# One core, FFN–attention–FFN: all five engines in source order, side work in small steps, table entries by indirect writes, value products two key tiles at a time

## The chip, the cores and the metric

The kernel runs on one core of one Trainium2 chip. Times are device microseconds (us) of one launch. A profiled execution also gives a trace, in which every instruction of the five engines (TensorE = PE, VectorE = DVE, ScalarE = ACT, GpSimd = POOL, SyncE = SP) has a start and an end.

## The reference, cut to what matters

The input x has 4 batches of 512 tokens and 256 features. One layer is computed, in fp32:

```
x = x + 0.5 * ffn(layernorm(x))
x = x + attention(layernorm(x))
x = x + 0.5 * ffn(layernorm(x))        # the same weights as the first

ffn(x):   logits = x @ gate             # 8 experts
          w, e = top_2(logits); w = softmax(w)
          out = sum over the two e of  w * ((silu(x @ w0[e]) * (x @ w1[e])) @ wo[e])   # 256 -> 512 -> 256

attention(x):   # 16 heads of 64 plain + 64 rotary dimensions
          q   = rms_norm(x @ wq_a) @ wq_b          # rank 64
          c,r = split(x @ wkv_a)                   # rank 64, and 64 rotary dimensions common to all heads
          k,v = split(rms_norm(c) @ wkv_b)
          rope on q's rotary part and on r
          out = softmax(q.k / sqrt(128)) @ v, heads side by side, @ wo
```

## The kernel before

**Three stages.** The first FFN, the attention and the second FFN follow each other. The up and key projections of the heads are folded into the queries and the value projection into the output weights ahead of time (`fold_pieces`), so that keys and values of all heads are the low-rank rows of the batch.

**FFN.** A token and one of its two experts make a pair; there are 4096 pairs. Each expert's pairs are put into slots, 128 slots make a tile of one expert, and 39 tiles (`NTILES`) hold every possible split. A table `tab` (slot within the tile by tile: token and weight) says which pair lies in which slot. To route a batch, the kernel normalises its rows (`norm`, L317), stores them to DRAM (`xn_d`), transposes them, multiplies with the gate, chooses two experts (`top_two`), numbers the slots (`slots`), and adds every pair to the table: for each of 8 groups of 128 pairs, three one-hot tiles (L609 on POOL, L613 on DVE) and a matmul (`put`, L624). `list_pieces` then lists the tiles that are full, and after the last batch the rest. Batches 0 and 1 are routed at the start (`route_first`, with all 16 one-hot groups in `p_put`), which fills `n_a` = 9 tiles; batches 2 and 3 are routed beside these tiles. In the second FFN, batches 0 to 2 are routed beside the attention (17 tiles), and batch 3 beside the first of these.

For each tile `ffn_tiles` (L746) gathers 128 rows by an indirect DMA (L760, POOL), transposes them (L772, to xT by DVE at L775), makes the two hidden products (`hidden`, L790, 8 matmuls; Silu on ACT, product on DVE at L802), transposes that (L808), projects it (L817), scales it by the pair's weight (L827, DVE) and adds it into the result `acc_d` in DRAM by an indirect DMA that accumulates (L832, POOL).

**Attention.** 64 items (batch, head) of 4 query tiles and 4 key tiles (`NT` = 4) each. `before_pieces` (L882) prepares a batch: norm, transposes, rotary keys (L896), low-rank rows (L911) with an RMS norm, and their transposes (L940). `queries` (L952) makes the queries of two heads, with `rope` (L870): two DVE and three POOL operations. `scores` (L966) makes one 128x512 tile of scores on PE (L969), its row maximum on DVE (L977), the exponential with row sums on ACT (L980), the reciprocal on DVE (L981) and the division on POOL (L982). `turn_probs` (L985) transposes the probabilities of one key tile `kc` (L989; copied to SBUF by DVE or ACT in turn). `weigh` (L999) multiplies one key tile of two heads with the values into `po` (L1002, 64 columns wide). `out_project` (L1010) projects two pairs of heads and adds them to x (L1016).

The main loop (L1162 to L1178) goes through items and key tiles. At each it issues the scores five tiles ahead (`LEAD` = 1), the transposes of this tile, and then, by the key tile, a `weigh`, the queries of a later pair, or half an output projection. At `kc` 1 a hook runs a piece of side work: one of the pieces of routing (9 to a batch) or of preparing (6 to a batch).

**What sets the order.** PE and SP run in source order (`manual_schedule(engines={PE, SP})`, L110). DVE, ACT and POOL are ordered by the tile scheduler, which may move an instruction of side work before or behind those of the main work on the same engine. Roots are taken on ACT (L313 for LayerNorm, L922 for RMS norm), which has to load a table of functions between Sqrt and Exp or Silu. DMAs that SP issues stand in one queue: after the first-layer weights it loads wo's weights (L1075, 4 MB), then x of batches 2 and 3 (L1077), `mark_d`, the start of `acc_d`, and the attention's weights (`load_attention`, L227), among them `nwq`, which DVE scales by a constant (L241).

Of the kernel before, what the change touches and what calls it, by code (L numbers as in the profile page):

```python
# [9 lines left out]
F32 = mybir.dt.float32  # L10
# [22 lines left out]
def kernel(  # L33
# [49 lines left out]
    xp = ctx.enter_context(tc.tile_pool(name="xn", bufs=4))  # L83
    lp = ctx.enter_context(tc.tile_pool(name="lT", bufs=1))
    qp = ctx.enter_context(tc.tile_pool(name="q", bufs=3))
    pp = ctx.enter_context(tc.tile_pool(name="p", bufs=2 * NT + LEAD))
    ptp = ctx.enter_context(tc.tile_pool(name="pt", bufs=NT + 2))
    ap = ctx.enter_context(tc.tile_pool(name="o", bufs=2))
    dp = ctx.enter_context(tc.tile_pool(name="dram", bufs=1, space=bass.MemoryType.DRAM))
    ps_a = ctx.enter_context(tc.tile_pool(name="ps_a", bufs=4, space=PSUM))  # L90
    ps_t = ctx.enter_context(tc.tile_pool(name="ps_t", bufs=2, space=PSUM))
    ps_p = ctx.enter_context(tc.tile_pool(name="ps_p", bufs=2, space=PSUM))
# [4 lines left out]

    mark_d = dp.tile([P, n_full(2)], F32, name="mark_d")
# [11 lines left out]
    order = {mybir.EngineType.PE, mybir.EngineType.SP}  # L110
    ctx.enter_context(tc.manual_schedule(engines=order))
# [76 lines left out]
    for t in (xn_d[0], acc_d[0], xn_d[1], acc_d[1]):  # L188
        nc.gpsimd.dma_start(t[NTOK:, :], zero)
# [112 lines left out]

    H2 = NT // 2

    def stats(b):

        mv = small.tile([P, NT, 2], F32, tag="mv", name="mv")
        for t in range(NT):
            sb = small.tile([P, 6], F32, tag="st", name="st")
            nc.vector.bn_stats(sb, xs[b][:, t, :])  # L310
            nc.vector.bn_aggr(mv[:, t, :], sb)
        rstd = small.tile([P, NT], F32, tag="rstd", name="rstd")
        nc.scalar.activation(rstd, mv[:, :, 1], AF.Sqrt, bias=eps_ln)  # L313
        nc.vector.reciprocal(rstd, rstd)
        return mv, rstd

    def norm(b, store=None, alone=False):  # L317

        xt = xs[b]
        mv, rstd = stats(b)  # L320
        if alone:
            less = small.tile([P, NT], F32, tag="less", name="less", bufs=2)
            nc.vector.scalar_tensor_tensor(
                less, mv[:, :, 0], -1.0, rstd, ALU.mult, ALU.mult
            )
        halves = []
        for half in range(2):
            xn = xp.tile([P, H2, D], F32, tag="xn", name="xn")
            for i in range(H2):
                t = half * H2 + i  # L330
                if alone and half:
                    nc.scalar.activation(
                        xn[:, i, :], xt[:, t, :], AF.Identity,
                        bias=less[:, t : t + 1], scale=rstd[:, t : t + 1],
                    )
                    continue
                eng = nc.gpsimd if i and not alone else nc.vector
                eng.tensor_scalar(
                    xn[:, i, :], xt[:, t, :], mv[:, t, 0:1], rstd[:, t : t + 1],
                    ALU.subtract, ALU.mult,  # L340
                )
            if store is not None:
                queue, dst = store
                r0 = b * S + half * H2 * P
                queue.dma_start(
                    dst[r0 : r0 + H2 * P, :].rearrange("(t p) d -> p t d", p=P), xn
                )
            halves.append(xn)
        return halves

    def turn_norm(halves):

        xnT = tp.tile([P, DC, S], F32, tag="xnT", name="xnT")
        for half, xn in enumerate(halves):
            pt = ps_p.tile([P, DC, H2 * P], F32, tag="p", name="pt_ln")
            for c in range(DC):
                for t in range(H2):
                    nc.tensor.transpose(  # L358
                        pt[:, c, t * P : (t + 1) * P], xn[:, t, c * P : (c + 1) * P], ident
                    )  # L360
            nc.scalar.copy(xnT[:, :, half * H2 * P : (half + 1) * H2 * P], pt)
        return xnT


    class Phase:


        def __init__(self, f):
            self.f = f

            self.run = rt.tile([P, NE], F32, name=f"run{f}")
            nc.gpsimd.memset(self.run, 0.0)

            self.tab = rt.tile([P, 2, P], F32, tag="tab", name="tab")
            self.in_a = None

    def own(name, shape, dt=F32, bufs=3):

        return small.tile(shape, dt, tag=name, name=name, bufs=bufs)

    def top_two(ph, pg, nt, mk):


        def bcast(v):
            return v.unsqueeze(2).to_broadcast([P, nt, NE])

        lg = mk("lg", [P, nt, NE], bufs=2)
        nc.vector.tensor_copy(lg, pg[:, :, :NE])
        hot = mk("hot", [P, 2, nt, NE], bufs=2)
        wgt = mk("wgt", [P, 2, nt])  # L390
        tops = []
        for k in range(2):
            m = mk(f"m{k}", [P, nt])
            nc.vector.tensor_reduce(m, lg, AX.X, ALU.max)
            eq = mk("eq", [P, nt, NE], bufs=2)
            nc.vector.tensor_tensor(eq, lg, bcast(m), ALU.is_equal)
            nc.vector.tensor_mul(eq, eq, rank[:, :nt])
            rm = mk("rm", [P, nt])
            nc.vector.tensor_reduce(rm, eq, AX.X, ALU.max)
            nc.vector.tensor_tensor(hot[:, k], eq, bcast(rm), ALU.is_equal)  # L400
            tops.append(m)
            if k == 0:
                lg2 = mk("lg2", [P, nt, NE], bufs=2)
                nc.vector.scalar_tensor_tensor(
                    lg2, hot[:, k], -BIG, lg, ALU.mult, ALU.add
                )
                lg = lg2

        both = mk("both", [P, 2, nt, NE], bufs=2)
        nc.vector.tensor_add(both[:, 0], hot[:, 0], hot[:, 1])  # L410
        nc.vector.tensor_copy(both[:, 1, 0, :], ph.run)
        for t in range(nt):
            nc.vector.tensor_add(
                both[:, 1, t + 1, :] if t + 1 < nt else ph.run,
                both[:, 1, t, :],
                both[:, 0, t, :],
            )

        ex = mk("ex", [P, nt])
        nc.vector.tensor_sub(ex, tops[1], tops[0])  # L420
        nc.scalar.activation(ex, ex, AF.Exp)
        den = mk("den", [P, nt])
        nc.vector.tensor_scalar_add(den, ex, 1.0)
        nc.vector.reciprocal(den, den)

        nc.vector.tensor_scalar_mul(wgt[:, 0], den, 0.5)
        nc.vector.tensor_mul(wgt[:, 1], ex, wgt[:, 0])
        return {"hot": hot, "wgt": wgt, "both": both}

    def slots(s, b, nt, mk):  # L430

        pr = ps_p.tile([P, nt, NE], F32, tag="p", name="pr")
        for i, m in enumerate((below, ones)):
            nc.tensor.matmul(  # L434
                pr.rearrange("p t e -> p (t e)"),
                lhsT=m,
                rhs=s["both"][:, i].rearrange("p t e -> p (t e)"),
                start=(i == 0),
                stop=(i == 1),
            )  # L440
        sv = mk("sv", [P, nt, NE], bufs=2)
        nc.vector.tensor_add(sv, pr, base[:, :nt])
        mine = mk("mine", [P, 2, nt, NE], bufs=2)
        nc.vector.tensor_mul(
            mine, s["hot"], sv.unsqueeze(1).to_broadcast([P, 2, nt, NE])
        )
        sl = mk("sl", [P, 2, nt])
        nc.vector.tensor_reduce(sl, mine, AX.X, ALU.add)
        s_i = mk("s_i", [P, 2, nt], I32)
        nc.vector.tensor_copy(s_i, sl)  # L450
        lo_i = mk("lo_i", [P, 2, nt], I32)
        nc.vector.tensor_single_scalar(lo_i, s_i, P - 1, ALU.bitwise_and)
        hi_i = mk("hi_i", [P, 2, nt], I32)
        nc.vector.tensor_single_scalar(hi_i, s_i, 7, ALU.arith_shift_right)
        lo = mk("lo", [P, 2, nt])
        nc.vector.tensor_copy(lo, lo_i)
        hi = mk("hi", [P, 2, nt])
        nc.vector.tensor_copy(hi, hi_i)
        val = mk("val", [P, 2, nt])
        nc.vector.scalar_tensor_tensor(  # L460
            val, tok_id[:, :, :nt], float(b * S), lo, ALU.add, ALU.subtract
        )
        return {"lo": lo, "hi": hi, "val": val}

    def route_first(ph, queue):

        s = {}
        nt = 2 * NT
        used = [0]

        def scratch(name, shape, dt=F32, bufs=0):
            if "scr" not in s or used[0] + math.prod(shape[1:]) > S:
                s["scr"] = pp.tile([P, S], F32, tag="p", name="scr")
                used[0] = 0
# [11 lines left out]
        def p_norm(b):  # L486
            s["xn", b] = norm(b, (queue, xn_d[ph.f]), True)
# [771 lines left out]
```

## Time and profile before

| | |
|---|---|
| time of 3 runs: median (lowest to highest) | 1213.18 us (1211.97 to 1214.32) |
| time of the profiled execution | 1212.9 us |
| its span (first to last instruction) | 1211.1 us |
| mean granted TensorE clock | 0.979 |
| first FFN: hidden products of tile 0 start at | 43.83 us |
| hidden products of tile 8 start at | 120.58 us |
| attention | about 318 to 968 us |
| second FFN | about 968 us to the end |
| queries to queries, a pair of heads without side work | 16.56 us; with an output projection 19.71 us |

The page gives the busy time of each engine over the whole span and in 40 equal slices, and the chain of instructions that ended last. Timelines give start, duration, engine, line and operation, and in brackets how long the engine had been idle and what released it. "SPq" is the time that an instruction took to be issued by SP's queue, not its transfer. In the trace a transposing matmul is one record and an fp32 matmul with 512 columns two. A block's "slot" below is the time from the start of its first matmul to the start of the next block's, since the ends of matmuls overlap.

### The profile page before, as it was taken

What the parts mean: (1) busy time and instruction counts of PE and PEld (TensorE: products, weight loads), DVE (VectorE), ACT (ScalarE), POOL (GpSimd) and SP (SyncE); (2) the same over time, 40 slices, a digit from 0 to 9 for tenths busy, and PEclk for the clock granted to TensorE, in tenths of its full rate; (3) what the DMA queues carried; (4) which work ended last, traced back from release to release, by engine and by line L of the source; (5) the groups of instructions that cost most, each with busy time, mean ns of one, the idle gap of its engine ahead of it and who ended that gap; (6) DMA issues with size and microseconds to landing.
All of it is one profiled execution on the core that took longest, in us unless ns stands there. A gap on an engine that the chain in (4) does not pass through costs nothing. (4 is left out here: it accounts for less than half of the span.)

```text
span 1211.1 us, 15165 instructions
## 1 busy us (share of the span) xinstructions
PE 1142.1 (94%) x4788; PEld 641.9 (53%) x4788; DVE 611.1 (50%) x1615; ACT 489.1 (40%) x1023; POOL 593.9 (49%) x631
## 2 busy tenths in 40 slices
PE   5599999899899999999999999999999899999996
PEld 4366666566545454445454445544555466666664
DVE  6355222333356565676566685666866435322221
ACT  4341221332355455645556644556544431122111
POOL 3265444455455545456555465455644335344352
PEclk7899999989999999999999999999999999999998
DMA  9941222322100000100001000001000122222431
GB/s 319 367 98 30 44 44 48 70 38 40 20 1 1 1 1 1 53 1 1 1 1 49 4 1 1 1 1 35 1 1 1 45 48 36 44 44 45 113 53 22
DMA packets 40334, 52.12 MB, mean 43 GB/s; under 512 B 9376, under 2 KB 32672, under 8 KB 40160
## 3 DMA queue, kind: packets, MB, share of 16 engines
q0 software_dynamic: 15808, 23.08, 10.8%
q1 hardware_dynamic: 24176, 28.06, 7.2%
q8 instruction: 41, 0.67, 0.2%
q14 instruction: 37, 0.30, 0.1%
q10 hardware_dynamic: 272, 0.01, 0.0%
HBM read 34.09 MB, written 21.24 MB: 46 GB/s over the span
## 5 line engine op out<-in xcount | busy, mean ns | idle before, releaser
L982 POOL TENSOR_SCALAR pr<-pr,sm 128x512 f32<-128x512 f32 x256 | 176.6, 696 | 232.9 <-DVE sm L981 192.9
L790 PE MATMUL h<-w_sb,xT 128*128 x624 | 286.5, 602 | 1.9 <-DVE xT L775 1.5
L969 PE MATMUL ps<-k,q 128*128 128x512 f32 x512 | 275.1, 621 | 0.0
L980 ACT ACTIVATE pr<-ps,nm 128x512 f32<-128x512 f32 x256 | 176.2, 689 | 178.6 <-DVE nm L977 145.5
L989 PEld LDWEIGHTS pt<-ident,pr 128*128 128x128 f32 x1024 | 129.0, 142 | 161.7 <-issue 114.8
L977 DVE TENSOR_REDUCE nm<-ps 128x1 f32<-128x512 f32 x256 | 175.5, 686 | 73.3 <-PE ps L969 72.6
L832 POOL DMA_INDIRECT acc_d<-yo,idx x64 | 101.8, 1590 | 192.9 <-DVE yo L827 176.6
L989 PE MATMUL pt<-ident,pr 128*128 128x128 f32 x1024 | 159.4, 276 | 20.1 <-POOL pr L982 18.3
L790 PEld LDWEIGHTS h<-w_sb,xT 128*128 128x128 f32 x624 | 114.5, 193 | 120.3 <-issue 118.7
L802 DVE TENSOR_TENSOR it<-g,h 128x512 f32<-128x512 f32 x78 | 53.6, 687 | 239.5 <-PE h L790 192.6
L810 ACT COPY iT<-pt_i 128x512 f32<-128x512 f32 x78 | 45.7, 585 | 258.7 <-PE pt_i L808 258.7
L817 PE MATMUL py<-w_sb,iT 128*128 x624 | 147.7, 380 | 0.7 <-ACT iT L810 0.7
L1002 PE MATMUL po<-pT,low 128*64 128x512 f32 x512 | 142.8, 623 | 1.2 <-ACT pT L996 1.2
L969 PEld LDWEIGHTS ps<-k,q 128*128 128x128 f32 x512 | 81.6, 192 | 91.2 <-issue 72.5
L817 PEld LDWEIGHTS py<-w_sb,iT 128*128 128x128 f32 x624 | 112.7, 190 | 14.4 <-issue 1.4
L996 ACT COPY pT<-pt 128x512 f32<-128x512 f32 x128 | 74.7, 583 | 84.9 <-PE pt L989 84.4
L760 POOL DMA_INDIRECT xg<-xn_d,idx x78 | 77.9, 998 | 30.4 <-issue 18.9
L994 DVE COPY pT<-pt 128x512 f32<-128x512 f32 x128 | 87.1, 681 | 10.5 <-PE pt L989 10.5
L800 ACT ACTIVATE g<-h 128x512 f32<-128x512 f32 x78 | 46.6, 597 | 103.5 <-PE h L790 103.4
L981 DVE RECIPROCAL sm<-sm 128x1 f32<-128x1 f32 x256 | 40.9, 160 | 91.5 <-ACT pr L980 91.4
L827 DVE TENSOR_SCALAR yo<-py,wt 128x256 f32<-128x256 f32 x78 | 37.7, 484 | 65.0 <-PE py L817 65.0
L876 POOL TENSOR_TENSOR tsin<-tsin,sin_sb 128x512 f32<-128x512 f32 x36 | 45.7, 1271 | 36.9 <-DVE tsin L875 36.9
(249 smaller groups left out, 1211.4 us busy)
## 6 DMA issues: line engine op xcount, KB each, us to landing
w_sb<-in_L_ffn_w_kernel_dram SPq DMA_DIRECT2D x8, 1024.0 KB, 17.3
w_sb<-in_L_ffn_wo_kernel_dram SPq DMA_DIRECT2D x4, 1024.0 KB, 13.8
x<-_attn_hidden_states_dram SPq DMA_DIRECT2D x4, 512.0 KB, 7.0
xn_d<-xn POOLq DMA_DIRECT2D x8, 256.0 KB, 5.7
x<-acc_d SPq DMA_DIRECT2D x4, 512.0 KB, 3.7
acc_d<-x SPq DMA_DIRECT2D x4, 512.0 KB, 2.9
xn_d<-xn SPq DMA_DIRECT2D x8, 256.0 KB, 2.3
out_dram<-acc_d SPq DMA_DIRECT2D x4, 512.0 KB, 5.7
```

Source lines behind the costliest of these rows:

```text
L760: nc.gpsimd.indirect_dma_start(out=xg[j], out_offset=None, in_=xn_d[f][: res["rows"], :], in_offset=bass.IndirectOffsetOnAxis(ap=res["idx" ...
L790: nc.tensor.matmul(p, lhsT=xT[j][:, c, :], rhs=w_sb[w][:, bass.ds(off + c * MLP, MLP)], start=(c == 0), stop=(c == DC - 1),)
L817: nc.tensor.matmul(py, lhsT=iT[:, m, :], rhs=w_sb[2][:, bass.ds(off + m * D, D)], start=(m == 0), stop=(m == MC - 1),)
L832: nc.gpsimd.indirect_dma_start(out=dst, out_offset=bass.IndirectOffsetOnAxis(ap=idx, axis=0), in_=y, in_offset=None, compute_op=ALU.add,)
L969: nc.tensor.matmul(ps, lhsT=qT[:, t * P : (t + 1) * P], rhs=st[b]["k"][h % 2], start=True, stop=True,)
L977: nc.vector.tensor_reduce(nm, ps, AX.X, ALU.max, negate=True)
L980: nc.scalar.activation(pr, ps, AF.Exp, bias=nm, accum_out=sm)
L982: nc.gpsimd.tensor_scalar(pr, pr, sm, 1.0, ALU.mult, ALU.mult)
L989: nc.tensor.transpose(pt[:, t * P : (t + 1) * P], probs[t][:, kc * P : (kc + 1) * P], ident)
L994: nc.vector.tensor_copy(s, pt)
L996: nc.scalar.copy(s, pt)
L1002: nc.tensor.matmul(po[j * RANK : (j + 1) * RANK], lhsT=st[b]["low"][:, kc, 1, :], rhs=pts[j], start=(kc == 0), stop=(kc == NT - 1),)
```

## The change

All five engines run in source order (`engines=None`). So an instruction of side work stands on each engine exactly where the source issues it, and everything behind it on that engine waits while it waits.

Side work is written as generators that stop after a few instructions; a queue, `Beside`, takes one step at fixed places: four places in a tile of the FFN (before: one), one or two in a key tile of the attention. In the first FFN the routing of batches 2 and 3 takes 3 steps a place beside tiles 0 and 1 and 2 steps beside tiles 2 to 6; what is left is done at the end of tile 6.

```diff
-    order = {mybir.EngineType.PE, mybir.EngineType.SP}
-    ctx.enter_context(tc.manual_schedule(engines=order))
+    ctx.enter_context(tc.manual_schedule(engines=None))
...
     for j in tiles:
-        for f in hooks.pop(j, ()):
-            f()
-        if j == len(jobs) - 1:
-            put_scores(0)
-            put_scores(1)
+        place = place + 1 if place < 4 else 1
+        if j < n_a - 2:
+            beside.step(3 if j < 2 else 2)
+            if j == n_a - 3 and place == 4:
+                beside.finish()
```

Roots: the Sqrt of ACT and the reciprocal become a bit trick with three Newton steps, 11 small DVE operations, for every norm but the first two. Normalised rows are made by DVE and ACT, no longer by POOL.

```diff
+    def inv_sqrt(y, x, n):
+        nc.vector.tensor_single_scalar(
+            y.bitcast(I32), x.bitcast(I32), 1, ALU.arith_shift_right
+        )
+        nc.vector.tensor_scalar(
+            y.bitcast(I32), y.bitcast(I32), -1.0, float(0x5F3759DF), ALU.mult, ALU.add
+        )
+        a = small.tile([P, n], F32, tag="newton", name="newton")
+        for i in range(3):
+            nc.vector.scalar_tensor_tensor(a, y, -0.5, x, ALU.mult, ALU.mult)
+            nc.vector.tensor_mul(a, a, y)
+            nc.vector.scalar_tensor_tensor(y, a, 1.5, y, ALU.add, ALU.mult)
```

The table: a pair's two numbers (8 bytes) go to their slot in a table in DRAM, `tab_d`, by an indirect DMA from POOL, 128 pairs at a time; once all are written, SP reads the table back (128 KB). Batches 0 and 1 of the first FFN keep the 16 one-hot groups; batches 2 and 3 use 8 writes and 8 one-hot groups (all three one-hots on DVE); each batch of the second FFN uses 8 writes.

```diff
+        def scatter(self, s, k, t):
+            nc.gpsimd.memset(self.between, 0.0)
+            put = nc.gpsimd.indirect_dma_start(
+                out=tab_d[self.f],
+                out_offset=bass.IndirectOffsetOnAxis(ap=s["s_i"][:, k, t : t + 1], axis=0),
+                in_=s["pair"][:, k, t, :],
+                in_offset=None,
+            )
```

The attention's loop: `at` counts the 8 key tiles of a pair of heads. `weigh` takes two key tiles at a time; the division is issued at a place of its own; queries and `rope` are taken in steps (`asked`): queries' matmuls at 5, the first rotary DVE operation at 6, the second at 7, and POOL's three at 0 (product), 1 (upper half, behind the division) and 2 (lower half) of the next pair, whose first scores stand at 3.

```diff
+            at = NT * (h % 2) + kc
+            k = (i + 1) * NT + LEAD + kc
+            put_scores(k)
             pts[i, kc] = turn_probs(probs[i], kc)
-            if kc == 0 and h % 2 == 0 and i > 0:
-                put_weigh(i - 1, NT - 1)
-            if kc > 0 and h % 2 == 1:
-                put_weigh(i, kc - 1)
-            if kc == 2 and h % 2 == 1:
-                put_queries((i + 3) // 2)
-            if kc >= 2 and h % 4 == 0 and i > 0:
-                put_out(i - 1, kc - 2)
-            if kc == 1:
-                for f in hooks.pop((b, h), ()):
-                    f()
+            for f in late:
+                f()
+            late.clear()
+            if at == 1 and i > 0:
+                put_weigh(i - 1, (2, 3))
+            elif at == 7:
+                put_weigh(i, (0, 1))
+            elif at == 3 and h % 4 == 0 and i > 1:
+                late.append(put_out(i - 1, 0))
+            elif at == 4 and h % 4 == 1 and i > 1:
+                late.append(put_out(i - 2, 1))
+                late.append(lambda i=i: finish_x(i - 2))
+            elif at == 5:
+                asked.add(put_queries((i + 3) // 2))
+            if kc % 2:
+                beside.step()
+            else:
+                asked.step()
+            put_divide(k)
+            if kc % 2:
+                asked.step()
+                if at in (1, 7):
+                    beside.step()
+            else:
+                beside.step()
```

Smaller edits: the first two score tiles of the attention are no longer issued before the last projection of the first FFN; x of batches 2 and 3 is loaded before wo's weights; the PSUM pool of scores, hidden products and `po` has 3 buffers instead of 4, that of side work 3 instead of 2; SBUF pools are cut anew. The scaling of `nwq`, which in the source stands ahead of the first tile's xT, is not edited; on DVE it now runs at that place.

## The prediction, as put on record

> **What bounds the kernel now.** I read the page's busy shares and slices first, then the waits of PE, then PE's timeline where the slices dip.
>
> ```profile
> PE 1142.1 (94%) x4788; PEld 641.9 (53%) x4788; DVE 611.1 (50%) x1615; ACT 489.1 (40%) x1023; POOL 593.9 (49%) x631
> ...
> PE   5599999899899999999999999999999899999996
> ```
>
> PE is busy 94% of the span and no other engine over 50%. A change can win by taking work off PE or by filling its gaps, and lose by opening new gaps: a 20 us gap costs 1.6%. The dips are slices 1 and 2 and a few single ones. The table of stretches gives the size:
>
> ```profile
> 43.80:120.60 76.80, 64.34 (x273) 39.84 (x274) 38.58 (x160) 20.70 (x32) 36.36 (x37) 0.91 0.47 129
> ...
> 334.00:968.00 634.00, 614.49 (x2666) 311.28 (x2664) 409.26 (x1012) 340.85 (x766) 334.17 (x392) 0.99 0.03 9
> 968.00:1198.00 230.00, 228.88 (x896) 143.42 (x897) 70.87 (x178) 48.94 (x82) 100.45 (x81) 1.00 0.29 53
> ```
>
> (Columns: stretch, length, busy PE, PEld, DVE, ACT, POOL, clock, DMA share, GB/s.) PE idles 12.5 us in tiles 0 to 7 of the first FFN, 19.5 us in the attention, 1.1 us in the second FFN. What ends these gaps:
>
> ```profile
> PE pt L989 <- POOL pr L982: 18.3, 14, 2.8
> PE pt_ln L494 <- DVE xn L338: 9.0, 1, 9.0
> PE pt_ln L358 <- DVE xn L338: 9.0, 1, 9.0
> PE pt_i L808 <- DVE it L802: 8.0, 5, 3.7
> ```
>
> In the attention PE waits for divided probabilities, 14 times up to 2.8 us. One such place, ACT first, then PE:
>
> ```profile
> 505.70 1.28 ACT L313 ACT_TABLE_LOAD   x1
> 507.00 0.30 ACT L313 ACTIVATE rstd<-mv,eps_ln 128x4 f32<-128x4 f32 x1
> 507.31 1.28 ACT L980 ACT_TABLE_LOAD   x1
> 508.61 0.69 ACT L980 ACTIVATE pr<-ps,nm 128x512 f32<-128x512 f32 x1
> ```
> ```profile
> 510.49 0.33 PE L989 MATMUL pt<-ident,pr 128*128 128x128 f32 x1 [2.63 <-POOL pr L982]
> ```
>
> A root costs ACT 2.9 us, the exponentials come late, and PE stands 2.63 us.
>
> **The change part by part**, against the profiled execution's 1212.9 us (the median of the runs, 1213.18, is 0.02% away).
>
> *1. Start of the first FFN.* DVE in source order meets the scaling of `nwq` (L241) right before xT of tile 0. Before, DVE's scheduler put it late:
>
> ```profile
> 43.83 5.37 PE L790 MATMUL h<-w_sb,xT 128*128 x8 [0.60 <-DVE xT L775]
> ```
> ```profile
> 60.08 2.98 SPq L240 DMA_DIRECT2D nwq<-n_L_attn_q_a_norm_w_dram  x2
> ...
> 69.51 0.14 DVE L241 TENSOR_SCALAR nwq<-nwq 128x1 f32<-128x1 f32 x1
> ```
>
> SP issues its two loads at 60 to 63 us, a median 5.2 us before they land: 65 to 68. Behind the scaling on DVE stand xT of tile 0, its product, and all statistics of batch 2; behind xT PE waits. SP's order ahead of `nwq` moves the same bytes, so the loads won't be earlier. Tile 0 starts at about 68.3 instead of 43.8: +24.5. Given back: the old wait of 9.0 us in tile 1 for batch 2 (x landing at 55.7, behind wo's weights) is gone. That leaves about +13 if tiles 0 to 7 otherwise keep pace, which is my lower bound.
>
> I don't expect them to. The routing of two batches and the listing are some 60 steps, 3 or 2 at each of 4 places a tile, ending in tile 6, and PE's part of a step waits in order for DVE's. I walked the emitted order with durations of rows: DVE carries about 31 us of side work (statistics 0.41 + 0.17 a tile of rows, choice 7.5, 24 one-hots at 0.28 to 0.47, table sums, listing), each round a trip PE to DVE and back. The walk puts tile 8 at 148 us against 120.58: +28. It charges every round trip in full, so I take the middle, **+20** (13 to 28). Half of the 16 one-hot groups' matmuls are already off in it.
>
> *2. Rest of the first FFN.* Tiles 8 to 38 at 5.82 us (hidden 3.44, projection 1.73, transposes 0.44 and 0.22) need 180.4; preparing batch 0 takes 6.1 of PE and queries 2.1; together 189. Now they take 318 − 120.6 = 197.4. The two waits at 229 to 247 (stretch: 18.0 us, PE 12.2) stem from Sqrt loads and POOL's rows (1278 ns each) ahead of gathers, which go. In steps, one a place, PE waits little: **−7** (−8 to 0).
>
> *3. Attention.* (a) *Switching to 64-wide matmuls.* In a block of four `po` records the two heads lie side by side in the two halves of the array's columns, so it streams as many columns as one score tile; it takes a slot of 1.01 against the score tile's 0.86; the scores' slot after it is 0.96 instead of 0.86, and the transposes' before it 0.53 instead of 0.44. A visit costs 0.15 + 0.10 + 0.09 = 0.35. One double block stands in the trace, 1.87 instead of 2.02. Four visits a pair become two: 0.70 × 32 pairs = **−22.4** (−16 to −22.4).
>
> (b) *The upper half of the rotary queries.* It now stands on POOL behind the division of tile 1, and the next pair's first scores at tile 3 wait for it. From the start of tile 1's scores: scores 0.6, maximum 0.69, exponential 0.69 + 0.19, reciprocal 0.16, hand-overs of 0.1 to 0.2 each, division 0.70, add 1.27: about 4.8 to 6.8 depending on what DVE holds. PE is there after tile 1 (0.86 + 0.53 + 1.87) and tile 2 (0.96 + 0.44, and waits for tile 2's own chain), about 6.1. I take 0.75 a pair: 32 × 0.75 = **+24** (0 to 35: at most 1.1 a pair). POOL's row for rope's operations:
>
> ```profile
> L876 POOL TENSOR_TENSOR tsin<-tsin,sin_sb 128x512 f32<-128x512 f32 x36 | 45.7, 1271 | 36.9 <-DVE tsin L875 36.9
> ```
>
> (c) *Roots off ACT.* Of the 19.5 us of idle PE most stands around the roots; the row maxima still meet the 11 Newton operations on DVE in order (row L311's 172 ns each, 2 us, in two steps). I take 60% of 21 us (the idle time plus slow clock after it): **−12.6** (−21 to 0).
>
> The Trainium skill, "ScalarE: Activation LUTs", section "What ACT_TABLE_LOAD costs", counts a drain of about 1.38 us with each 1.28 us load; here the exponential follows its load at 507.31 by 1.30 us, so no drain shows. By the page the term could be twice as large; the row decides.
>
> (d) *Table matmuls* of three batches: 12 blocks (L624) with slots of 0.86 to 0.97 go: **−11** (certain as PE time; by idle elsewhere it may be hidden: −11 to 0).
>
> (e) *Indirect writes*: 8 a batch, 24 here. The trace has none of 8 bytes a row. From below the gather's 998 ns of POOL, from above the adding write's 1590:
>
> ```profile
> L832 POOL DMA_INDIRECT acc_d<-yo,idx x64 | 101.8, 1590 | 192.9 <-DVE yo L827 176.6
> ...
> L760 POOL DMA_INDIRECT xg<-xn_d,idx x78 | 77.9, 998 | 30.4 <-issue 18.9 <-DVE off L739 4.8 <-PE po L1002 4.4
> ```
>
> I take 1.4 with its small memset, nearer the write. Queued behind each on POOL are the division and rope; whoever is late there is the next pair's scores. Also, rope's add in a batch's first pairs waits for writes to land (3.8 us for `acc_d` <- `yo`). POOL's busy share in the attention is 53%, so half of it hides: 8 × 1.4 = 11 a batch, of which I charge 5: **+15** (0 to 18).
>
> The skill, "DMA: Bandwidth & Descriptors", table "Specifications", says transfers below 512 bytes are read, modified and written, which speaks against 8-byte writes. No row here has such a transfer; the one other case is the adding write, which also reads first.
>
> (f) *Side steps on DVE in order* hold a row maximum back by about half an operation of 0.69, in 28 of 32 pairs: 0.35 × 28 = **+10** (0 to 10).
>
> (g) *Start.* No scores are issued before the last projection, and five first tiles run max, exp, reciprocal in turn on DVE: now about 6 us are lost at 318 to 334: **+3** (0 to 4).
>
> Attention: −22.4 + 24 − 12.6 − 11 + 15 + 10 + 3 = **+6** (−35 to +30, since not all ends come together).
>
> *4. Second FFN.* Four table blocks of batch 3 go: **−3.5** (−3.5 to 0). Its tiles already run at 5.83, near their floor.
>
> Buffers: the pool of scores with 3 costs nothing by itself in the FFN (two hidden products in use, 3.44 us, freed by 0.69 of DVE); in the attention it is part of (b).
>
> **Sum**: 1212.9 + 20 − 7 + 6 − 3.5 = 1228.4.
>
> **Rivals.**
>
> *A, the other side: the chain behind POOL keeps up.* If the upper half is ready before PE reaches tile 3 (it decides at 6.1 us from tile 1's start; DVE must be free when each maximum comes) and the writes hide in POOL's idle 47%, (b), (e) and (f) vanish: 1228.4 − 24 − 15 − 10 = 1179. For it: POOL idles 193 us before divisions, waiting for DVE, not the reverse. Against: DVE is 65% busy in the attention (409 of 634 us) and in order now.
>
> *B, worse: the chain is late in every pair* and writes cost the upper price: (b) 35, (e) 18, start +28: 1228.4 + 11 + 3 + 8 = 1250.
>
> *C, grouping does nothing:* if slots around a double block pay the switch twice, (a) is 0 and the time is about 1228.4 + 22 = 1250, unless (b) is gone too: 1226.
>
> *D, the hold at the start is not there* (`nwq` lands by 50): 1228.4 − 20 = 1208.
>
> **How the numbers follow.** Forecast and its near surroundings (1210 to 1245): 0.45. A: 0.26. B and C at 1250: 0.20. D: 0.09. The range takes in A's 1179 and B's 1250 with some margin: 1177 to 1256. The likeliest case's own range is 1210 to 1245. 0.2% (2.4 us) is about what a measurement of this kernel can tell from no change. Faster: A and half of D, 0.31; within 0.2%: the rest of D and 0.01 of the forecast's lower end, 0.05; slower: 0.64.
>
> **What would show it.** Right or wrong by the profile of the changed kernel: tile 0's hidden products start at 65 to 70 us, released by DVE's xT, behind `nwq` (else term 1 fails); tile 8 starts at 134 to 149. A clean pair, queries to queries, at 16.4 to 16.6 as before says (a) and (b) cancel; at 15.8 rival A holds; PE's waits would name the rotary queries' upper half at the scores' line with about 24 us. `po` blocks of eight records with slots near 1.87 show (a). No table loads between 330 and 960 but for Exp. The 24 writes show their POOL slot directly. I would be wrong mostly if the in-order DVE is not late at the row maxima.

## The result, and the profile after

The changed kernel is slower: 1306.95 us median (1296.25 to 1309.77, 4 runs) against 1212.58, a ratio of 1.0755 (95% interval 1.0700 to 1.0811). The profiled execution took 1296.25 us (span 1294.5), the fastest of the four; the other three have a mean granted clock of 0.947 to 0.948 instead of its 0.959. A fifth execution on record, not in this median, took 1301.42 us at 0.956.

The page of the changed kernel, busy time and slices:

```profile
PE 1133.8 (88%) x4704; PEld 642.0 (50%) x4704; DVE 617.1 (48%) x1673; ACT 452.2 (35%) x992; POOL 578.2 (45%) x645
...
PE   5367899999889999897989879898879998999996
```

PE has 8.3 us less work than before and 91.7 us more idle time in its span. Slices 2 and 3 are deeper, and dips stand all over the attention. The stretches (columns as in the prediction): tiles 0 to 7, attention, first 17 tiles of the second FFN.

```profile
66.70:153.70 87.00, 66.16 (x252) 39.83 (x253) 37.80 (x148) 15.44 (x26) 28.47 (x33) 0.88 0.20 34
...
346.28:1034.58 688.30, 612.04 (x2632) 318.02 (x2630) 421.33 (x1078) 321.67 (x761) 334.49 (x412) 0.97 0.03 8
1034.58:1150.25 115.67, 106.35 (x414) 65.78 (x414) 37.20 (x122) 24.02 (x40) 47.60 (x46) 0.97 0.30 45
```

| | before | after | difference |
|---|---|---|---|
| start to tile 8 of the first FFN | 120.58 | 153.70 | +33.1 |
| tile 8 to the attention's first scores | 197.55 | 192.58 | −5.0 |
| attention (to the second FFN's first product) | 645.3 | 688.3 | +43.0 |
| second FFN, tiles 0 to 16 | 107.4 | 115.7 | +8.3 |
| its tiles 17 to 38 and the end | 140.2 | 144.2 | +4.0 |

These are the two profiled executions, and the differences come to 83.4 us; of the 94.4 us between the medians, 11 lie in executions without a trace.

The waits of PE name new causes at the top; what led before (PE for the division, 18.3 us) is down to 3.2:

```profile
PE ps L1100 <- POOL q L1001: 56.2, 30, 8.1
PE pt_ln L381 <- DVE xn L367: 23.7, 8, 8.4
PE h L907 <- DVE xT L892: 21.6, 3, 20.5
...
PE pt L1122 <- POOL pr L1116: 3.2, 5, 1.2
```

**The start.** DVE's timeline, then PE's:

```profile
66.03 0.15 DVE L247 TENSOR_SCALAR nwq<-nwq 128x1 f32<-128x1 f32 x1 [26.54 <-DMA nwq<-n_L_attn_q_a_norm_w_dram]
66.13 0.42 DVE L892 COPY xT<-pt_x 128x256 f32<-128x256 f32 x1
```
```profile
66.65 2.05 PE L907 MATMUL h<-w_sb,xT 128*128 x2 [20.46 <-DVE xT L892]
```

DVE stands 26.5 us before an operation of 0.15 us whose result is first read at 311 us, more than 200 us later; the copy behind it releases PE.

**A clean pair of the attention**, POOL's timeline, then PE's:

```profile
462.87 0.70 POOL L1116 TENSOR_SCALAR pr<-pr,sm 128x512 f32<-128x512 f32 x1 [0.98 <-PE po L1135]
463.65 1.26 POOL L1001 TENSOR_TENSOR q<-tcos,tsin 64x512 f32<-64x512 f32 x1
```
```profile
459.50 1.02 PE L1100 MATMUL ps<-k,q 128*128 128x512 f32 x2
...
463.72 0.60 PE L1122 MATMUL pt<-ident,pr 128*128 128x128 f32 x4
464.97 1.12 PE L1100 MATMUL ps<-k,q 128*128 128x512 f32 x2 [0.64 <-POOL q L1001]
```

The upper half's add follows the division at once; PE waits 0.64 us for it, in every clean pair. From the start of place 1's scores (459.50) to that of place 3's (464.97) it is 5.47 us. Clean pairs take 16.67 and 20.12 us against 16.56 and 19.71.

**A pair with indirect writes**, the same two views:

```profile
580.43 1.04 POOL L441 DMA_INDIRECT tab_d<-cut  x1 [0.16 <-DMA tab_d<-cut]
581.48 0.12 POOL L440 MEMSET between<- 128x1 f32 x1
581.78 0.97 POOL L441 DMA_INDIRECT tab_d<-cut  x1 [0.19 <-issue]
582.79 0.70 POOL L1116 TENSOR_SCALAR pr<-pr,sm 128x512 f32<-128x512 f32 x1
587.34 1.25 POOL L1001 TENSOR_TENSOR q<-tcos,tsin 64x512 f32<-64x512 f32 x1 [3.86 <-DMA tab_d<-cut]
```
```profile
588.65 2.08 PE L1100 MATMUL ps<-k,q 128*128 128x512 f32 x2 [8.06 <-POOL q L1001]
590.52 1.06 PE L1122 MATMUL pt<-ident,pr 128*128 128x128 f32 x4
```

The same add doesn't start until the last of five writes has landed, 4.6 us after that write's end on POOL, and PE stands 8.06 us. Then it runs at half clock (2.08 for 1.12, 1.06 for 0.60). In the trace the semaphore waits on these writes, one for each of the five then in flight from POOL, carry the line of the upper half's add; the lower half's add behind it has none. In the kernel before the upper half's add carries waits for indirect DMAs too, at the end of the first FFN, though there it came behind the lower half's; between 325 and 956 us POOL issued no DMA, so in the attention there was nothing to wait for. So coming first isn't what makes the wait. The add differs from the lower half's in its partitions, 64 to 127; why it carries the wait stays open.

### The profile page after: what moved, and what is told of

Its sections match the earlier page's. It is cut to its first block, busy times and chain, and to the rows that moved or that the text cites. A ratio compares the mean times of both kernels' runs of the same rounds, so it can differ in the third digit from the quotient of the medians.

```text
span 1294.5 us, 15127 instructions
## 1 busy us (share of the span) xinstructions
PE 1133.8 (88%) x4704; PEld 642.0 (50%) x4704; DVE 617.1 (48%) x1673; ACT 452.2 (35%) x992; POOL 578.2 (45%) x645
## 5 line engine op out<-in xcount | busy, mean ns | idle before, releaser
L1100 PE MATMUL ps<-k,q 128*128 128x512 f32 x512 | 285.3, 641 | 60.5 <-POOL q L1001 56.2
L1122 PEld LDWEIGHTS pt<-ident,pr 128*128 128x128 f32 x1024 | 131.6, 145 | 146.7 <-issue 122.9
L934 PE MATMUL py<-w_sb,iT 128*128 x624 | 151.0, 386 | 1.3 <-ACT iT L927 1.3
L1135 PE MATMUL po<-pT,low 128*64 128x512 f32 x512 | 123.9, 605 | 0.0
L1115 DVE RECIPROCAL sm<-sm 128x1 f32<-128x1 f32 x256 | 41.2, 161 | 115.7 <-ACT pr L1111 115.3
L1149 PE MATMUL pwo<-wvo,oT 128*128 128x256 f32 x256 | 61.5, 383 | 0.1
## 6 DMA issues: line engine op xcount, KB each, us to landing
w_sb<-in_L_ffn_wo_kernel_dram SPq DMA_DIRECT2D x4, 1024.0 KB, 13.2
```

The costliest lines, as they stand in the source:

```text
L934: nc.tensor.matmul(py, lhsT=iT[:, m, :], rhs=w_sb[2][:, bass.ds(off + m * D, D)], start=(m == 0), stop=(m == MC - 1),)
L1100: nc.tensor.matmul(ps, lhsT=qT[:, t * P : (t + 1) * P], rhs=st[b]["k"][h % 2], start=True, stop=True,)
L1122: nc.tensor.transpose(pt[:, t * P : (t + 1) * P], probs[t][:, kc * P : (kc + 1) * P], ident)
L1135: nc.tensor.matmul(po[j * RANK : (j + 1) * RANK], lhsT=st[b]["low"][:, kc, 1, :], rhs=pts[j], start=(kc == 0), stop=(kc == NT - 1),)
```

## Experiments

Times are medians; ratios are to the kernel before in the same session (1211.2 to 1213.5 us). The changed kernel itself was timed in another session only, and the interval of its ratio is 6.7 us to either side: differences from its 1306.95 us are no better than that, while lengths of stages come from profiled executions.

**nwq_late**: the scaling moved behind the load of x for batch 1, just ahead of the preparation's queue.

```diff
-        nc.vector.tensor_scalar_mul(nwq, nwq, scale)
...
             load_x(1, rows(acc_d[0], 1))
+            nc.vector.tensor_scalar_mul(nwq, nwq, scale)
```

> The changed kernel, with the scaling of nwq issued where batch 0's preparation begins instead of ahead of tile 0's xT. Theory (DVE in source order is held by two late loads): tile 0's hidden products start near 44 us instead of 66.7, the 87 us from tile 0 to tile 8 stay about as they are, so tile 8 starts near 131 instead of 153.7 and the time falls by about 22 us. Rival (the pace of the routing's steps and the loads of x set tile 8, the hold only hides in them): tile 8 stays above 145 and the time falls by less than 9 us.

Measured: 1280.49 us, 1.0561 (1.0542 to 1.0581), 26.5 below the changed kernel. Tile 0 starts at 47.6, tile 8 at 130.6. The theory holds; 83.0 us from tile 0 to tile 8 remain, 6.3 more than before. PE's waits for the normalised rows of the batches routed there are as long as in the changed kernel, which comes first here:

```profile
78.02 1.23 PE L381 MATMUL pt_ln<-ident,xn 128*128 128x128 f32 x4 [6.00 <-DVE xn L367]
92.19 0.78 PE L381 MATMUL pt_ln<-ident,xn 128*128 128x128 f32 x4 [3.46 <-DVE xn L367]
```
```profile
57.50 1.23 PE L380 MATMUL pt_ln<-ident,xn 128*128 128x128 f32 x4 [6.01 <-DVE xn L366]
70.44 1.13 PE L380 MATMUL pt_ln<-ident,xn 128*128 128x128 f32 x4 [3.46 <-DVE xn L366]
```

**hi_dve**: the upper half's add on DVE.

```diff
-        nc.gpsimd.tensor_add(hi, tcos[ROPE:], tsin[ROPE:])
+        nc.vector.tensor_add(hi, tcos[ROPE:], tsin[ROPE:])
```

> The changed kernel, with the add of the upper half of rope on DVE instead of POOL. Theory (PE waits 56.2 us at the first scores of a pair for this add, which on POOL stands behind a division and, after indirect writes, waits for them to land): the wait goes, clean pairs take about 16.0 us instead of 16.67, the first pairs of a batch with writes about 17 to 19 instead of 25, and the time falls by 45 to 56 us. Rival (side work in source order on DVE and ACT makes these pairs late, and the wait is only where it shows): clean pairs gain, the others don't, and the time falls by 10 to 15 us.

Measured: 1270.05 us, 1.0473 (1.0453 to 1.0493), 36.9 below the changed kernel. Clean pairs take 15.88 and 19.21 us; the pair with most of the writes 21.59 instead of 25.67. The attention falls from 688.3 to 654.9. Between the two: the wait is a cause, but 19 us of the 56 come back elsewhere, in part as waits for divisions behind writes on POOL (11.7 us, named by the write's memset):

```profile
PE pt L1122 <- POOL between L440: 11.7, 6, 2.9
PE pt_x L889 <- DMA xg<-xn_d,idx: 8.1, 4, 4.4
PE pn_c L778 <- DVE wide L775: 6.7, 4, 2.8
```

**hi_first**: the add still on POOL, issued ahead of the division at place 1.

```diff
+            if at == 1:
+                asked.step()
             put_divide(k)
             if kc % 2:
-                asked.step()
+                if at != 1:
+                    asked.step()
```

> The changed kernel, with the add of the upper half still on POOL, but issued ahead of the division of its key tile instead of behind it. Theory (two separate causes: place behind the division, and the wait for indirect writes): clean pairs fall from 16.67 to about 16.0, the waits of 7 to 8 us in the pairs with writes stay, and the time falls by 8 to 15 us. Rival (the division's place doesn't matter, another chain ends last in a clean pair): clean pairs stay at 16.67, within 3 us.

Measured: 1272.54 us, 1.0498 (1.0477 to 1.0520), 34.4 below the changed kernel, more than expected. Clean pairs take 15.89 us, so the place behind the division was worth 0.78 a pair. The long waits at the scores (8.14, 7.29 and 6.92 us) stay, those of 2 to 3 us go: the add's second wait of a batch and those in pairs of preparation hung on the place, not on the writes.

```profile
PE ps L1100 <- POOL q L1001: 22.6, 4, 8.1
```

So nearly all that hi_dve gains comes from the place. The attention takes 658.4 us here, 29.9 less than in the changed kernel. Taking out the three long waits as well, as hi_dve does, shortens the pairs in which they stand by 11.2 us in all (26.36, 24.89 and 24.65 us here; 21.59, 21.57 and 21.53 there), but the attention by 3.5 only: the rest comes back in other pairs.

**one_kc**: one key tile at a time, at the places of the kernel before.

```diff
-            if at == 1 and i > 0:
-                put_weigh(i - 1, (2, 3))
-            elif at == 7:
-                put_weigh(i, (0, 1))
+            if at == 0 and i > 0:
+                put_weigh(i - 1, (3,))
+            if at > 4:
+                put_weigh(i, (at - 5,))
```

> The changed kernel, with the value products one key tile at a time again, at the places where they were before. If the grouping saves PE what two visits of 0.35 us cost a pair and all of it reaches the end: 22 us slower. Theory (in the changed kernel a clean pair ends with a wait of 0.64 us at the scores, which takes up most of what PE saves): clean pairs within 0.3 us of 16.67, the time 0 to 10 us slower. If grouping saves nothing: no change.

Measured: 1368.86 us, 1.1282 (1.1263 to 1.1301), 62 above the changed kernel; clean pairs 20.52. All three readings fall. In its trace the wait at the scores of place 3 grows to 2.32 us, and in most clean pairs the granted clock is 0.5 for 3.4 us after it. This led to a fourth reading: the double product at place 1 stands between the scores of place 1, which start the chain maximum, exponential, reciprocal, division, upper half, and those of place 3, which wait for it. Work there is free; moved out, it is paid in full.

**three_visits**: tests that reading.

```diff
-            if at == 1 and i > 0:
-                put_weigh(i - 1, (2, 3))
+            if at < 2 and h % 2 == 0 and i > 0:
+                put_weigh(i - 1, (2 + at,))
```

> The changed kernel with the second value product cut in two, key tile 2 at place 0 and key tile 3 at place 1; the first stays double at place 7. Three readings of the run one_kc, in which a clean pair took 20.52. Theory (from the scores of place 1 to those of place 3 the chain through the upper half's add has a fixed length, and PE's work at places 1 and 2 is hidden in it; what is moved out is paid in full): 1.1 us of work moves out, the wait at the scores grows from 0.64 to about 1.5, clean pairs 17.7. Rival (the PSUM buffer of the value products, held longer, leaves two for scores): held as long as in the changed kernel, so clean pairs at most 17.0. Rival (each visit costs 1.9 us): 18.6.

Measured: 1315.25 us, 1.0832 (1.0804 to 1.0861); clean pairs 17.49, the wait 1.11 in them.

```profile
478.41 1.13 PE L1100 MATMUL ps<-k,q 128*128 128x512 f32 x2
...
483.59 1.12 PE L1100 MATMUL ps<-k,q 128*128 128x512 f32 x2 [1.11 <-POOL q L1001]
```

The time is nearest to the fixed chain (17.7) and excludes the two rivals (at most 17.0; 18.6); the wait grew by 0.47, half of what was expected. The chain is nearly fixed: from the scores of place 1 to those of place 3 it takes 5.18 us here and 5.18 in one_kc, against 5.47 in the changed kernel. The 0.82 us that a pair is longer are these 0.47 and one more visit (0.35).

**before_two**: the grouping alone, in the kernel before, with one more buffer for transposed probabilities and one fewer for normalised rows.

```diff
-            if kc == 0 and h % 2 == 0 and i > 0:
-                put_weigh(i - 1, NT - 1)
-            if kc > 0 and h % 2 == 1:
-                put_weigh(i, kc - 1)
+            if kc == 0 and h % 2 == 0 and i > 0:
+                put_weigh(i - 1, 2)
+                put_weigh(i - 1, 3)
+            if kc == 2 and h % 2 == 1:
+                put_weigh(i, 0)
+                put_weigh(i, 1)
```

> The kernel before with one part alone: value products two key tiles at a time (at the first and the seventh key tile of a pair), seven buffers for transposed probabilities instead of six, three for normalised rows instead of four. If two visits fewer a pair are worth what their slots show (0.35 us each) and nothing else ends last there: clean pairs 15.9 instead of 16.56, the time 16 to 22 us lower. Rival (the value product's PSUM buffer or the probabilities now end last): clean pairs 16.4 or more, the time within 5 us.

Measured: 1201.40 us, 0.9922 (0.9905 to 0.9938). Clean pairs take 15.87; the attention 625.7 instead of 645.3, −19.6, as the slots said. The first FFN lost 7 (first scores at 325.1).

**before_roots**: the Newton roots alone, in the kernel before, all but the first two norms (diff as in the change).

> The kernel before with one part alone: roots by Newton steps on DVE, with DVE still ordered by the scheduler. If ACT's table loads made the gaps of 19.5 us in the attention and part of the 9 us at 229 to 247 us: 12 to 25 us lower. Rival (the eleven small DVE operations delay the row maxima as much): within 5 us.

Measured: 1211.12 us, 0.9998 (0.9987 to 1.0009): nothing. No table is loaded in the attention for a root, and yet:

```profile
315.55:961.65 646.10, 622.70 (x2689) 315.57 (x2687) 430.73 (x1108) 325.00 (x758) 340.13 (x398) 0.99 0.03 8
```

PE idles 23.4 us there (before: 22.6). DVE has 17 us more work, and PE's waits shift from the division (18.3 to 11.2) to copies by DVE (5.4) and the low-rank rows (3.7).

**before_both**: the two together.

> The kernel before with both: value products two key tiles at a time and roots by Newton steps. If they add: 28 to 45 us below the kernel before, so 1168 to 1185 us. Rival (with PE's work gone, the chain through DVE, ACT and POOL ends the pairs with side work): less than the sum of the two alone by 8 us or more.

Measured: 1201.51 us, 0.9919 (0.9902 to 0.9935), the same as before_two: with nothing from the roots there is nothing to add.

**free_order**: the changed kernel with DVE, ACT and POOL ordered by the scheduler.

```diff
-    ctx.enter_context(tc.manual_schedule(engines=None))
+    order = {mybir.EngineType.PE, mybir.EngineType.SP}
+    ctx.enter_context(tc.manual_schedule(engines=order))
```

> The changed kernel with one part undone: DVE, ACT and POOL ordered by the scheduler again (PE and SP in source order). Theory (source order on DVE and POOL makes most of the loss): tile 0's hidden products start at 44 to 48 us, the upper half's add is no longer late, the time falls by 60 to 100 us. Rival (the steps, the indirect writes and the shared buffers cost it): it falls by less than 30 us.

Measured: 1257.23 us, 1.0371 (1.0348 to 1.0394), 49.7 below the changed kernel, between the two. Tile 0 starts at 45.1. But the pairs with most of the writes take 33.3 to 34.5 us: now the scheduler puts the waiting add ahead of divisions on POOL.

```profile
544.21 1.01 POOL L442 DMA_INDIRECT tab_d<-cut  x1 [0.17 <-issue]
552.59 1.27 POOL L1002 TENSOR_TENSOR q<-tcos,tsin 64x512 f32<-64x512 f32 x1 [7.37 <-issue]
```

**twice**: hi_dve, each write repeated into a table nobody reads.

```diff
             self.written.append(put)
+            nc.gpsimd.memset(self.between, 0.0)
+            again = nc.gpsimd.indirect_dma_start(
+                out=tab_x[self.f],
...
```

> The run hi_dve with each indirect write issued twice, the second time to a table that nobody reads: 40 more writes, 24 of them in the attention. If a write costs its slot on POOL and half of that is hidden, as predicted (1.2 to 1.4 us): 13 to 17 us more in the attention. If POOL's idle time hides it: within 4 us. If writes collide on their way (each waits for others to land): 30 us or more.

Measured: 1298.80 us, 1.0716 (1.0672 to 1.0759), 28.8 above hi_dve. The attention grows from 654.9 to 671.5: 16.6 us for 24 writes, 0.69 each, half of the slot of 1.3 us (memset 0.10, write 0.98, gaps). This is the price of a second write beside the first, with the add on DVE.

**two_six**: the grouping in the kernel before with no buffer changed; at the seventh key tile the product is issued ahead of the transposes.

```diff
             put_scores((i + 1) * NT + LEAD + kc)
+            if kc == 2 and h % 2 == 1:
+                put_weigh(i, 0)
+                put_weigh(i, 1)
             pts[i, kc] = turn_probs(probs[i], kc)
+            if kc == 0 and h % 2 == 0 and i > 0:
+                put_weigh(i - 1, 2)
+                put_weigh(i - 1, 3)
```

> The kernel before with value products two key tiles at a time, as in the run before_two, but with no buffer changed: at the seventh key tile of a pair the product of key tiles 0 and 1 is issued ahead of the transposes, so six buffers are enough. If the buffers of normalised rows cost the earlier run its first FFN (tile 0 at 49.9 instead of 43.8, first scores at 325 instead of 318): tile 0 back at about 44, first scores at 318, clean pairs 15.87, 1189 to 1195 us. Rival (the product ahead of the transposes makes PE wait for copies of probabilities): clean pairs above 16.2, 1198 us or more.

Measured: 1200.56 us, 0.9906 (0.9889 to 0.9922). The first FFN is back (first scores at 318.1), but clean pairs take 16.03 and some pairs with side work 1.2 to 1.8 us more than in before_two (19.51 for 18.26, 19.73 for 17.96); the attention is 632.1 us, −13.2. Neither reading fits fully.

**two_six_x**: two_six, and x of batches 2 and 3 loaded ahead of wo's weights.

```diff
+    for b in range(2, B):
+        load_x(b, x_in(b))
     load_expert_weights(2)
-    for b in range(2, B):
-        load_x(b, x_in(b))
```

> The run two_six with one more part of the change: x of batches 2 and 3 loaded before wo's weights. If the wait of 9.0 us in tile 1 is for x alone: tile 8 starts 5 to 9 us earlier and the time falls by as much against two_six. Rival (the first projections wait for wo instead, or the rows behind x are late anyway): within 3 us of two_six.

Measured: 1191.27 us, 0.9823 (0.9807 to 0.9839), 9.3 below two_six: the fastest of all, faster than both kernels. The transposes of batch 2 in tile 1, which waited 8.96 us before, wait 0.56, and the projection that needs wo doesn't wait:

```profile
52.31 0.33 PE L358 MATMUL pt_ln<-ident,xn 128*128 128x128 f32 x1 [0.56 <-DVE xn L338]
...
58.35 1.89 PE L817 MATMUL py<-w_sb,iT 128*128 x8
```

**nwq_hi**: nwq_late and hi_dve together.

> The changed kernel with both mends, nwq's scaling late and the upper half's add on DVE. If the two causes are independent: 26 us below hi_dve, so 1241 to 1247 us, with tile 8 near 130 and the attention 655 us long. If they overlap: 1255 us or more.

Measured: 1240.65 us, 1.0207 (1.0156 to 1.0259): 66.3 below the changed kernel, against 26.5 + 36.9 = 63.4. Within what these medians can tell, they add (its four runs lie between 1231 and 1245 us).

**free_nwq_hi**: nwq_hi with the scheduler's order on DVE, ACT and POOL.

> The run nwq_hi with DVE, ACT and POOL ordered by the scheduler again. What is left against the kernel before (about 31 us) lies in pairs with side work, in tiles 0 to 7 and in the second FFN. If source order makes it: 20 to 40 us below nwq_hi. If the indirect writes and the side work's steps make it, whatever the order: within 8 us of nwq_hi.

Measured: 1214.04 us, 1.0002 (0.9990 to 1.0015), 26.6 below nwq_hi and level with the kernel before. The two executions' stretches to tile 8 and of the attention, nwq_hi first:

```profile
47.50:130.50 83.00, 63.08 (x252) 38.95 (x253) 37.87 (x148) 15.75 (x27) 28.54 (x33) 0.90 0.42 107
322.80:975.54 652.74, 608.97 (x2633) 315.34 (x2631) 445.07 (x1111) 321.79 (x761) 306.55 (x378) 0.97 0.03 9
```
```profile
44.80:123.50 78.70, 63.06 (x253) 38.27 (x254) 35.10 (x148) 15.49 (x27) 27.24 (x25) 0.91 0.50 126
319.75:954.24 634.49, 596.89 (x2633) 311.15 (x2631) 435.51 (x1093) 325.99 (x759) 306.87 (x355) 0.98 0.03 9
```

Source order costs 18.3 us of the attention, 4.3 of tiles 0 to 7, 2.7 ahead of them and 4.8 of the second FFN, and gains 4.0 between tile 8 and the attention. At the scheduler's order the attention is 10.8 us shorter than in the kernel before (634.5 for 645.3) and the second FFN 12.5 longer (260.1 for 247.6). That second loss isn't one of source order: here too a copy that begins the listing stands on DVE until POOL's DMAs, batch 3's writes among them, have landed, and PE waits behind it.

```profile
1006.64 0.23 DVE L775 COPY wide<-run 128x128 f32<-128x128 f32 x1 [15.18 <-DMA xg<-xn_d,idx]
```
```profile
1009.57 1.12 PE L925 MATMUL pt_i<-ident,it 128*128 128x128 f32 x4 [12.81 <-DVE it L919]
```

## Why the prediction was wrong

The sign and the two large mechanisms (DVE held behind `nwq`, the upper half's add late at the scores) were right; the sum was off: forecast 1228.4, range to 1256, measured 1307. Two steps failed: the sum of the attention, where a gain was booked that isn't there and three losses were each booked too low, and the 9 us booked as given back at the start.

1. *Start of the first FFN, +20 (13 to 28)*: +33.1. The hold was as told: tile 0 at 66.7, predicted 68.3, with DVE behind nwq. The return failed. I booked the old 9 us wait as given back and took the middle against my own walk, which put tile 8 at 148. The order of the loads alone does give 9 us back in the kernel before (two_six_x). In the changed kernel PE waits 6.0 and 3.5 us in these tiles for normalised rows, which DVE now makes in steps, and as long in nwq_late, where DVE isn't held. So tiles 0 to 7 take 10.3 us more than before, and 6.3 of that is there without the hold.
2. *Rest of the first FFN, −7*: −5.0, right. The roots alone give −3.9 there in the kernel before (before_roots, tile 8 to the first scores 193.7 for 197.6).
3. *Attention, +6 (−35 to +30)*: +43.0, the step that failed most.

| term | forecast | measured | from |
|---|---|---|---|
| (a) grouping | −22.4 | −19.6 | before_two |
| (b) upper half behind the division | +24 | +29.9 | changed kernel against hi_first |
| (c) roots off ACT | −12.6 | +0.8 | before_roots |
| (d) table matmuls | −11 | no run | |
| (e) indirect writes | +15 | 16.6 for POOL's slots, 3.5 more for the landing | twice; hi_first against hi_dve |
| (f) source order | +10 | 18.3, on DVE, ACT and POOL | nwq_hi against free_nwq_hi |
| (g) start | +3 | no run | |

With (d) and (g) as forecast the measured column comes to 41.5 of the 43.0. The terms are from different kernels, so that it comes so close is partly chance; but no single term makes the loss. The largest miss is (c), 13 us. I read the table loads off the chain of one stall; with them gone, DVE's copies and the low-rank rows end the same pairs. Whether the same holds in the changed kernel no run shows. Next is (f), 8 us, then (b), 6, and (e), 5.

In (b) 0.75 a pair was near (0.64 of wait, 0.78 of time), with some luck: I had PE at place 3's scores 6.1 us after place 1's, it was ready after 4.8 and the chain took 5.5. What was missing are the pairs with preparation, which waited 2 to 3 us. In (e) I named the landing and didn't add it. It made the longest single waits of PE, 7.3 to 8.1 us in each of three batches, with half clock after them, 22.7 us in all; yet hi_dve, without them, has an attention only 3.5 us shorter than hi_first. So the longest waits weren't the largest loss.

4. *Second FFN, −3.5*: +12.3. Four matmul blocks go, but the gathers stand behind batch 3's writes on POOL, and the copy that begins the listing waits on DVE until POOL's DMAs have landed:

```profile
1087.81 0.66 PE L889 MATMUL pt_x<-ident,xg 128*128 128x128 f32 x2 [4.08 <-DMA xg<-xn_d,idx]
1098.25 0.38 PE L778 MATMUL pn_c<-ones,wide 128*128 128x1 f32 x2 [1.57 <-DVE wide L775]
```
```profile
1097.97 0.23 DVE L775 COPY wide<-run 128x128 f32<-128x128 f32 x1 [5.57 <-DMA acc_d<-yo,idx]
```

I had priced the writes of this stage at nothing. The +4.0 of its tiles 17 to 38 and the end is not explained.

Rival A (the chain keeps up) is out; B was nearest, at 1250 still too low. C is out: grouping works in both kernels, in the changed one above all, since the double block hides the chain. D is out: nwq landed at 66 us. The PSUM pool of three buffers for scores and the new sizes of the SBUF pools were not run alone.

## What to carry to other kernels

When engines get source order, look for the operations whose inputs come late, and ask what is queued behind each: one scaling of 0.15 us cost 26 us, one add 37, of which 34 were its place behind a division. An operation that PE waits for has to stand ahead of work that isn't urgent. What a wait costs is shown only by a run without it: the three longest waits, 22 us in the profile, gave 3.5 us of the attention when they went. A part that pays alone (grouping, an earlier load) is best tried alone: the two together took the kernel before from 1212 to 1191 us, inside the change larger losses covered them.

## What was not expected of the hardware

*Gaps of 2 us can halve PE's clock.* In five traces with waits for the upper half (the changed kernel, nwq_late, hi_first, one_kc, three_visits), a score tile's first record took about 697 ns (full speed) after every gap up to 1.72 us and about 1220 ns (half) after every gap of 6 us and more; between 1.9 and 3.6 us both occur (at 2.08 to 2.09 us three of four were slow in the changed kernel's trace). The length of the one gap isn't all: in hi_dve and `twice`, single tiles after 0.69 us were slow as well (1193 and 1191 ns). In the changed kernel's attention the granted clock is 0.5 for 3.41 or 6.83 us at a time, 6.83 after each of the three long gaps. After the 8.06 us gap the next two blocks took 2.72 us instead of 1.40. In the second FFN the clock stayed at 1.00 after a gap of 1.57 us at `pn_c` in the profiled execution; after one of 2.81 in hi_dve's it was 0.74 over 20 us, which makes up some 5 of the 6.6 us between these two stretches (an estimate: 0.26 of 20 us). The difference among the changed kernel's own runs goes with their granted clocks (0.959 against 0.947), whose gaps no trace shows. The Trainium skill, "TensorE: Matmul & The Clock Gate", section "Part 1: The HAM clock gate", gives an idle window of about 3.4 us, free-running. The spread between 1.9 and 3.6 us agrees with a window that runs freely; the gaps of 2.08 us that halved the clock are shorter than the page's figure.

*Table loads off ACT bought nothing*: with the roots of all but two norms off ACT the kernel before ran in 0.9998 of its time. ACT was busy 347 of the attention's 645 us, and the pairs in which loads stood took about as long without them: those with the RMS norm's two loads 21.95 to 21.97 us before and 22.02 to 22.03 in before_roots, those with a LayerNorm's 22.13 and 22.08 before, 23.02 and 21.27 in before_roots.
